# The FFN product with W_base by Strassen's scheme over pairs of row tiles

## The chip, the cores and the metric

The kernel runs on one core of one Trainium2 chip. The metric is device time in microseconds (us) of one execution; lower is better. Before the change three timed runs took 767.62 us in the median (767.52 to 768.48).

Engine names below: PE is TensorE (matmul and transpose, PEld its weight loads), DVE is VectorE, ACT is ScalarE, POOL is GpSimd, SP is SyncE, which issues nearly all DMAs.

## The reference

One pre-norm transformer block on x of shape (2, 1024, 1024), float32: 2048 tokens, 1024 features.

```
x = x + attn(layernorm(x))        # convolution over 3 tokens -> q, k, v of width 256; 16 heads of 64;
                                  # causal softmax inside blocks of 128 tokens; wo; proj_w to 1024
x = x + ffn(layernorm(x))

ffn(x):  y      = x @ W_base.T + b_base                       # (2048 x 1024) @ (1024 x 1024)
         z_e    = x @ lora_A[e].T            (r = 8)          # for the 4 active experts
         logits = x @ router_W.T + router_b, active ones only
         alpha  = softmax(log(prior + eps) + logits)
         y      + sum_e alpha_e * 2 * (z_e @ lora_B[e].T)
```

The change is in the product with W_base and in what surrounds it.

## The kernel before

Every large product is made of three matmuls: each float32 operand is split into a rounded part "hi" and a rest "lo" (type fp32r), and hi·hi, hi·lo and lo·hi are added in PSUM. The helper `three` (matmul on L140) does this, so most matmuls of the trace carry the line L140 and are told apart by their tiles. A split costs one ACT copy (hi) and one DVE subtraction (lo).

The stages follow each other on PE: layer norm and transposes (tiles `xt`, `tr`), the convolution (`pm`), attention (`pq`, `pv`, scores `s`, transposes `pt`, `po`, `pw`), then the FFN stage. Attention works on 32 head pairs i, two at a time, in 16 rounds K of some 17 us. The FFN stage works on 16 row tiles g of 128 tokens in the order of the list `gs`, n being the place in it. For each tile:

- `load_xr` (DMA of x, 512 KB), `add_projb` (POOL, L1111), `project` (12 matmuls into `pp`), `residual` (DVE, L1126), statistics and `x_norm` (DVE, POOL for the root on L1136, DVE L1141), `transpose_x` (8 transposes `trx`, L1148), `x_hi` (ACT, L1155) and `x_lo` (DVE, L1159): this gives the split transposed tile `xT`, [128 features, 8 chunks, 128 tokens].
- `dense`: 8 chunks dc of 128 features, times three matmuls, times three column ranges of 354, 354 and 352 columns (`CUTS`): 72 matmuls into three PSUM banks `py`. The 1060 columns are the 1024 outputs and, in front of them, 36 columns for the four experts' lora_A rows and router row, so that z and the logits come out of the same matmuls.
- the gate (`gate_logits`, `gate_exp`, `gate`: small DVE and ACT operations), `transpose_z` (`pzt`, L1218), `z_out`, then `experts` (L1232): one matmul per column range adds lora_B and b_base.
- `add_y` (DVE, L1239) adds each bank to the row tile `xr`, and `store` writes it out.

W_base is needed in split form, 1060 columns by two parts for each of the 8 chunks. Six chunks are split during attention (rounds 12 to 14: `staged_hi` on L1071, `staged_lo` on L1075) and kept in DRAM (`wbd`); once the big buffers of attention are free (`big`, `wr0`, `wr1`), `load_staged` (L1083) reads them back, 1 MB each. The last two chunks are split at the start of the FFN stage. All eight stay in SBUF to the end.

The order of work on each engine is fixed when the program is built: every step is an `Op` with an engine, an estimated duration, a due time, the steps it comes after, and the buffers it takes and gives back (`places`: `m` are the 8 PSUM banks, `ml`, `t2`, `t4`, `a4`, `vh` are pools in SBUF). `trace()` plays this plan through and emits the steps in the order of their planned starts. On the chip each engine and SP's DMA queue then work strictly in that order.

Of the kernel before, what the change touches and what calls it, by code (L numbers as in the profile page):

```python
# [10 lines left out]
F32 = mybir.dt.float32  # L11
# [10 lines left out]
P = 128  # L22
# [17 lines left out]
def preln_block_kernel(  # L40
# [70 lines left out]
    BIG = max(NDC * N * (2 * J + 1), 2 * NWC * 2 * HD, 4 * 2 * (ZC + O))  # L111
# [481 lines left out]
    WR = max(2 * NWC * HD, 2 * 2 * (ZC + O))  # L593
# [454 lines left out]
    wb, wb_at = {}, {}  # L1048

    def open_wb(tag, dcs):  # L1050
        k = len(dcs)
        n = 2 * k * (ZC + O)
        t = big("wb0", (n,), FR) if tag == "big" else wr(tag, f"wb_{tag}")[:, :n]
        t = t.rearrange("p (h c f) -> p h c f", h=2, c=k)
        for c, dc in enumerate(dcs):
            wb[dc] = [t[:, h, c, :] for h in range(2)]
            wb_at[dc] = t, c

    def wb_hi(dc, h):
        nc.scalar.copy(wb[dc][0][:, ds(ZC + h * TC, TC)], raw["wb", dc, h])  # L1060

    def wb_lo(dc, h):
        hi, lo = (t[:, ds(ZC + h * TC, TC)] for t in wb[dc])
        nc.vector.tensor_tensor(lo, raw.pop(("wb", dc, h)), hi, ALU.subtract)


    wbd = [dram.tile([P, 2, O], F32, name=f"wbd{dc}") for dc in range(NDC - 2)]

    def staged_hi(dc, h):
        raw["hi", dc, h] = ml(f"wbhi_{dc}_{h}")[:, :TC].bitcast(FR)  # L1070
        nc.scalar.copy(raw["hi", dc, h], raw["wb", dc, h])  # L1071

    def staged_lo(dc, h):
        r = raw["wb", dc, h]
        nc.vector.tensor_tensor(r.bitcast(FR), r, raw["hi", dc, h], ALU.subtract)  # L1075

    def store_staged(dc, h, part):
        t = raw.pop((("hi", "wb")[part], dc, h))
        nc.sync.dma_start(wbd[dc][:, part, ts(h, TC)], t.bitcast(F32) if part == 0 else t)

    def load_staged(dc):
        tag, c = wb_at[dc]
        nc.sync.dma_start(tag[:, :, c, ZC:].bitcast(F32), wbd[dc])  # L1083

    za = ap_.tile([P, 2, EA, NDC * RA], FR, tag="za", name="za", bufs=1)

    def za_hi():
        nc.scalar.copy(za[:, 0], asel[:, :, : NDC * RA])

    def za_lo():  # L1090
        nc.vector.tensor_tensor(za[:, 1], asel[:, :, : NDC * RA], za[:, 0], ALU.subtract)

    def wz(dc):
        t, c = wb_at[dc]
        for h in range(2):
            nc.scalar.copy(
                t[:, h, c, :ZC].rearrange("p (e r) -> p e r", e=EA),
                za[:, h, :, ds(dc * RA, RA)],
            )
# [4 lines left out]
    xrs, xns, xTs, pps, trxs, mvs, rss, pys, zrs, zTs, pzts, gat = ({} for _ in range(12))  # L1104

    def load_xr(g):
        xrs[g] = a4(f"xr_{g}", (D,))
        nc.sync.dma_start(xrs[g], xr_of[g])
# [43 lines left out]
    def x_hi(g, h):  # L1152
        if h == 0:
            xTs[g] = [a4(f"xT{i}_{g}", (NDC, P), FR) for i in range(2)]
        nc.scalar.copy(xTs[g][0][:, ts(h, 4), :], trxs[g, h])  # L1155

    def x_lo(g, h):
        hi, lo = (t[:, ts(h, 4), :] for t in xTs[g])
        nc.vector.tensor_tensor(lo, trxs.pop((g, h)), hi, ALU.subtract)  # L1159


    CUTS = [(0, 354), (354, 708), (708, ZC + O)]
    LAST_CUTS = [(0, 402), (402, 804), (804, ZC + O)]

    def cut(n, k):
        return (LAST_CUTS if n == len(gs) - 1 else CUTS)[k]

    def dense(n, k, dcs):
        g = gs[n]
        a, b = cut(n, k)  # L1170
        if 0 in dcs:
            pys[g, k] = bank(f"py_{g}_{k}", (b - a,))
        for dc in dcs:
            three(
                pys[g, k],
                [t[:, dc, :] for t in xTs[g]],
                [t[:, a:b] for t in wb[dc]],
                dc == 0, k == 0 and dc == NDC - 1,
            )


    def gate_logits(g):
        pz = pys[g, 0][:, :ZC].rearrange("p (e r) -> p e r", e=EA)
        lg, al, a2 = (
            small.tile([P, EA], F32, tag=t, name=f"{t}_{g}") for t in ("lg", "al", "a2")
        )
        nm, asum, ar = (
            small.tile([P, 1], F32, tag=t, name=f"{t}_{g}") for t in ("nm", "asum", "ar")
        )
        nc.vector.tensor_tensor(lg, pz[:, :, R], lbias, ALU.add)  # L1190
        nc.vector.tensor_reduce(nm, lg, AX.X, ALU.max, negate=True)  # L1191
        gat[g] = pz, lg, al, a2, nm, asum, ar

    def gate_exp(g):
        pz, lg, al, a2, nm, asum, ar = gat[g]
        nc.scalar.activation(al, lg, AF.Exp, bias=nm, accum_out=asum)  # L1196

    def gate(g):
        pz, lg, al, a2, nm, asum, ar = gat.pop(g)
        nc.vector.reciprocal(ar, asum)  # L1200
        nc.vector.tensor_scalar(a2, al, ar, LORA_SCALING, ALU.mult, ALU.mult)
        zs = small.tile([P, ER], F32, tag="zs", name=f"zs_{g}")
        nc.vector.tensor_tensor(
            zs.rearrange("p (e r) -> p e r", r=R),
            pz[:, :, 0:R],
            a2[:, :, None].to_broadcast([P, EA, R]),
            ALU.mult,
        )

        zr = zrs[g] = small.tile([P, ZK], FR, tag="zr", name=f"zr_{g}")  # L1210
        nc.vector.memset(zr[:, 3 * ER :].bitcast(F32), 1.0)
        nc.vector.tensor_copy(zr[:, ts(0, ER)], zs)
        nc.vector.tensor_tensor(zr[:, ts(1, ER)], zs, zr[:, ts(0, ER)], ALU.subtract)
        nc.vector.tensor_copy(zr[:, ts(2, ER)], zs)

    def transpose_z(g):
        pzts[g] = bank(f"pzt_{g}", (P,), FR, rows=ZK)
        nc.tensor.transpose(pzts[g], zrs.pop(g), identr)  # L1218

    def z_out(g):  # L1220
        zTs[g] = small.tile([ZK, P], FR, tag="zT", name=f"zT_{g}", bufs=2)
        nc.scalar.copy(zTs[g], pzts.pop(g))

    def y_part(n, k):

        a, b = cut(n, k)
        py = pys[gs[n], k]
        return (py[:, ZC:], 0, b - ZC) if k == 0 else (py, a - ZC, b - ZC)

    def experts(n, k):  # L1230
        py, a, b = y_part(n, k)
        nc.tensor.matmul(  # L1232
            py, zTs[gs[n]], bb[:ZK, a:b], start=False, stop=True, skip_group_check=k == 0
        )

    def add_y(n, k):
        py, a, b = y_part(n, k)
        x2 = xrs[gs[n]]
        nc.vector.tensor_tensor(x2[:, a:b], py, x2[:, a:b], ALU.add)  # L1239
        pys.pop((gs[n], k))  # L1240

    def store(n, k=None):
        g = gs[n]
        a, b = (0, O) if k is None else (max(0, cut(n, k)[0] - ZC), cut(n, k)[1] - ZC)
        nc.sync.dma_start(or_of[g][:, a:b], xrs[g][:, a:b])
# [6 lines left out]
        m=[0.0] * 8, t2=[0.0] * 6, t4=[0.0] * 6, a4=[0.0] * A4, ml=[0.0] * 2, vh=[0.0] * 2  # L1252
# [97 lines left out]
    def plan_x(n, due):  # L1350
        g = gs[n]
        op(("X", n), DMA, 1.4, due - 12.0, [], partial(load_xr, g), lag=3.0, need=("a4",))
        op(("xb", n), POOL, 2.4, due - 4.0, [("X", n), ("pb",)], partial(add_projb, g))

    def plan_p(n):
# [3 lines left out]
        if ch < NCHUNK - 2 and g % NB == 0:  # L1359
            for wc in range(NWC):  # L1360
                op(("oh", ch, wc), DMA, 1.4, at[0] - 6.0, [("os", ch, wc)], partial(load_oh, ch, wc),
                   lag=3.0, need=("t4",))
                d["ol", ch, wc] = d["oh", ch, wc]
        for h in range(2):
            pe(("P", n, h), MM,
               [("ol", ch, wc) for wc in range(NWC)] + [("rl", "pw", wc, h) for wc in range(NWC)],
               partial(project, g, h), give=("t4",) * 2 if h and g % NB == NB - 1 else ())
# [6 lines left out]
    def plan_tx(n):  # L1374
        g = gs[n]
        for h in range(2):
            pe(("TX", n, h), 0.44, [("xn", n)], partial(transpose_x, g, h),
               give=("a4",) if h else ())
            op(("xh", n, h), ACT, 0.55, at[0] + 0.5, [("TX", n, h), ("xh", n, 0)],
               partial(x_hi, g, h),  # L1380
               need=("a4",) * 2 if h == 0 else ())
            op(("xl", n, h), DVE, 0.65, at[0] + 1.2, [("xh", n, h)], partial(x_lo, g, h),
               give=("m",))

    def after_dense(n, k, dc):
        return [("xl", n, dc // 4), ("rl", "wb", dc, 0), ("rl", "wb", dc, 1), ("wz", dc, 1)] + (
            [("Y", n, k, dc - 1)] if dc else [])

    def plan_dense(n, k, dcs):
        a, b = cut(n, k)  # L1390
        for dc in dcs:
            pe(("Y", n, k, dc), 3 * (b - a) * 0.000454, after_dense(n, k, dc),
               partial(dense, n, k, [dc]), need=("m",) if dc == 0 else (),
               give=("a4",) * 2 if (k, dc) == (2, NDC - 1) else ())
# [226 lines left out]
```

## Time and profile before

| | |
|---|---|
| median of three runs | 767.62 us |
| the profiled execution | 767.54 us, of which its span is 765.5 us |
| granted TensorE clock in it | 0.999 |
| PE busy | 756.6 us |
| DVE busy | 545.0 us |
| ACT busy | 400.5 us |
| POOL busy | 157.8 us |
| DMA | 100.19 MB, mean 131 GB/s |
| FFN stage, from the first `py` matmul to the end | 515.84 to 765.5 us |

The span runs from the first to the last instruction of the program. A group's busy time is the union of its instructions' times. A matmul's own duration contains its way through the array and overlaps the next one, so what one matmul costs is read from the time between starts (the chain of waits gives it for runs of equal matmuls). An engine can be busy all the time and still not be at its peak.

### The profile page before, as it was taken

To read this page: it belongs to the slowest core of one execution; us is meant where nothing else is said; L and a number is where in the kernel's file an instruction comes from. 1 tells how busy PE (TensorE), PEld (TensorE's weight loads), DVE (VectorE), ACT (ScalarE), POOL (GpSimd) and SP (SyncE) were. 2 spreads that over 40 slices of the span, in tenths; PEclk is the share of its full clock that TensorE was granted. 3 is DMA by queue.
4 is the path that set the end of the run, shared out by engine and by line. 5 is a ranking of instruction groups with operands and counts; after the bars stand their busy time and mean duration, and the time that the engine had idled before them with its cause. 6 is when DMAs were issued, how large, how long until landed. Compare 5 with 4: busy or idle time off the path is not lost.

```text
span 765.5 us, 13108 instructions
## 1 busy us (share of the span) xinstructions
PE 756.6 (99%) x4948; PEld 676.6 (88%) x4948; DVE 545.0 (71%) x1027; ACT 400.5 (52%) x1015; POOL 157.8 (21%) x138
## 2 busy tenths in 40 slices
PE   7999999999999999999999999999999999999998
PEld 7999988888888888888888887889999999999998
DVE  7888899889766998878887788687434454444532
ACT  6987337364837978887787989832101101010110
POOL 3224222210000322212122113442121111221000
PEclk9999999999999999999999999999999999999999
DMA  8937994994831121031031646750313112311011
GB/s 343 365 104 229 238 259 124 292 272 116 284 118 56 42 63 41 2 118 42 23 97 50 201 166 218 277 213 21 110 56 111 56 56 102 118 56 56 29 56 56
DMA packets 53663, 100.19 MB, mean 131 GB/s; under 512 B 4526, under 2 KB 23742, under 8 KB 53600
## 3 DMA queue, kind: packets, MB, share of 16 engines
q1 hardware_dynamic: 49872, 89.35, 33.2%
q0 software_dynamic: 3728, 10.00, 7.3%
q8 instruction: 39, 0.64, 0.3%
q14 instruction: 24, 0.20, 0.1%
HBM read 73.12 MB, written 26.21 MB: 130 GB/s over the span
## 4 chain that ended last, share of the span: by engine, by line
PE 95%; DVE 2%; DMA 1%; ACT 1%; issue 0%; POOL 0%; DVEq 0%
PE pm L140 26%; PE py L140 25%; PE pq L140 11%; PE pp L140 6%; PE pw L140 5%; PE pv L140 5%; PE s L904 4%; PE po L968 4%; PE pt L951 4%; PE trx L1148 2%; PE tr L385 1%; PE py L1232 1%; DVE lnst L132 1%; DMA xt<-in_x 1%; DMA wbd<-raw_wb 0%; DMA raw_pw<-in_proj_w 0%
## 5 line engine op out<-in xcount | busy, mean ns | idle before, releaser
L140 PE MATMUL pm<-v,u 128*128 128x256 f32 (+1 forms) x1152 | 203.1, 337 | 1.3 <-ACT v L473 0.9
L140 PEld LDWEIGHTS pm<-v,u 128*128 128x128 f32 x1152 | 177.9, 190 | 24.2 <-ACT v L473 1.2
L140 PE MATMUL py<-wb,xT 128*128 128x354 f32 (+3 forms) x576 | 120.4, 327 | 0.0
L140 PE MATMUL py<-wb_wr,xT 128*128 128x354 f32 (+3 forms) x576 | 118.1, 327 | 0.0
L944 POOL TENSOR_TENSOR p<-p,rs 128x1024 f32<-128x1024 f32 x32 | 61.5, 1926 | 251.5 <-DVE rs L940 204.0
L933 ACT ACTIVATE p<-p,nmx 128x128 f32<-128x128 f32 x256 | 99.4, 397 | 2.6 <-DVE nmx L928 2.5
L140 PEld LDWEIGHTS py<-wb_wr,xT 128*128 128x128 f32 x576 | 96.6, 188 | 2.4
L140 PEld LDWEIGHTS py<-wb,xT 128*128 128x128 f32 x576 | 96.6, 189 | 0.1
L140 PE MATMUL pq<-yt,wqk 128*128 128x512 f32 x384 | 94.3, 399 | 0.0
L140 PEld LDWEIGHTS pq<-yt,wqk 128*128 128x128 f32 x384 | 70.7, 188 | 18.4 <-issue 1.5
L1159 DVE TENSOR_TENSOR xT<-trx,xT 128x512 fp32r<-128x512 f32 x32 | 20.9, 686 | 56.0 <-PE trx L1148 49.1
L1155 ACT CAST xT<-trx 128x512 fp32r<-128x512 f32 x32 | 18.6, 588 | 63.7 <-POOL xr L1111 31.9
L1196 ACT ACTIVATE al<-lg,nm 128x4 f32<-128x4 f32 x16 | 4.8, 297 | 88.0 <-DVE nm L1191 88.0
L1111 POOL TENSOR_TENSOR xr<-xr,projb 128x1024 f32<-128x1024 f32 x16 | 38.4, 2398 | 60.1 <-DMA xr<-in_x 59.4
L933 ACT ACTIVATION_READ_ACCUMULATOR p<-p,nmx 128x1 f32 x256 | 50.0, 195 | 0.0
L919 DVE TENSOR_TENSOR p<-s,mask 128x512 f32<-128x512 f32 x64 | 41.6, 677 | 8.8 <-PE s L904 8.6
L140 PE MATMUL pw<-oT,wot 128*128 128x512 f32 x192 | 47.6, 396 | 0.0
L140 PE MATMUL pv<-wvt,yt 128*128 128x512 f32 x192 | 46.6, 392 | 0.0
L896 ACT ACTIVATE qk<-pq,bq 128x512 f32<-128x512 f32 x32 | 37.8, 1182 | 13.6 <-PE pq L140 13.6
L140 PEld LDWEIGHTS pw<-oT,wot 128*128 128x128 f32 x192 | 35.9, 188 | 8.5
L140 PEld LDWEIGHTS pv<-wvt,yt 128*128 128x128 f32 x192 | 36.1, 188 | 8.2
L445 DVE TENSOR_TENSOR u<-g,u 128x768 fp32r<-128x768 f32 x40 | 37.5, 951 | 1.4 <-ACT u L441 1.2
(161 smaller groups left out, 1196.4 us busy)
## 6 DMA issues: line engine op xcount, KB each, us to landing
g<-in_conv_w SPq DMA_DIRECT2D x48, 384.0 KB, 7.6
mdr<-m SPq DMA_DIRECT2D x36, 256.0 KB, 3.1
g<-in_conv_w POOLq DMA_DIRECT2D x24, 384.0 KB, 7.7
xt<-in_x SPq DMA_DIRECT2D x16, 512.0 KB, 9.7
xr<-in_x SPq DMA_DIRECT2D x16, 512.0 KB, 3.9
out<-xr SPq DMA_DIRECT2D x15, 512.0 KB, 2.9
ml<-mdr SPq DMA_DIRECT2D x18, 384.0 KB, 3.5
raw_wb<-in_w_base SPq DMA_DIRECT2D x16, 256.0 KB, 9.6
```

The costliest lines, as they stand in the source:

```text
L140: nc.tensor.matmul(ps, l[a], r[b], start=first and i == 0, stop=last and i == 2)
L445: nc.vector.tensor_tensor(lo, raws.pop((v, dc)), hi, ALU.subtract)
L896: nc.scalar.activation(out, pq, AF.Identity, bias=b_ap[:, hp : hp + 1], scale=sc)
L904: nc.tensor.matmul(s[j][:, b, :], qh[ts(j, DH), ts(b, P)], kh[ts(j, DH), ts(b, P)], start=True, stop=True,)
L919: nc.vector.tensor_tensor(ps[i][0][:, ts(j, NB), :], ss[i][j], mask[:, None, :].to_broadcast([P, NB, P]), ALU.add,)
L933: nc.scalar.activation(p[:, k, :], p[:, k, :], AF.Exp, bias=nmx[:, k : k + 1], accum_out=sm[:, k : k + 1],)
L944: nc.gpsimd.tensor_tensor(p, p, rs[:, :, None].to_broadcast([P, 2 * NB, P]), ALU.mult)
L951: nc.tensor.transpose(pt[:, ts(b, P)], ps[i][0][:, j * NB + b, :], ident)
L968: nc.tensor.matmul(po[ts(j, DH), ts(b, P)], vh[:, b, ds((i % 4) * P + j * DH, DH)], pT[:, j, ts(b, P)], start=True, stop=True,)
L1111: nc.gpsimd.tensor_tensor(xrs[g], xrs[g], pwt["b"], ALU.add)
L1155: nc.scalar.copy(xTs[g][0][:, ts(h, 4), :], trxs[g, h])
L1159: nc.vector.tensor_tensor(lo, trxs.pop((g, h)), hi, ALU.subtract)
```

## The change

The product of two row tiles (256 tokens, 1024 features) with W_base (1024 features, 1024 outputs) is cut into 2 by 2 blocks: A11, A12 are the first tile's two halves of features, A21, A22 the second's; B11 to B22 are the blocks of the weights, 512 by 512. Strassen's scheme (in Winograd's form) takes seven block products instead of eight, with sums of A blocks (S1 to S4) and differences of B blocks (T1 to T4). The stage now steps over eight pairs m.

- Each product is two half products of 6 matmuls, all 512 columns wide (`multiply_half`): 84 matmuls for a pair into the banks a, b, c, e. The products are A11·B11, S2·T2, A12·B21, S1·T1, S3·T3, S4·B22, A22·T4, in that order.
- S1 to S4 are made by DVE from the transposes in PSUM; A21 is copied to SBUF by ACT; seven operands of a pair are split (before: two tiles, four halves).
- The banks are combined: `u_first` copies bank a (ACT), `u_second` adds b (DVE), POOL adds the sum to three half rows of `xr` (`add_u`), and DVE adds bank e and bank c once more in the middle of their accumulation (`add_y` with last=False).
- z and the logits have products of their own (`z_products`): 32 matmuls for a pair with 72 or 36 weight columns and 128 moving columns, a copy to SBUF (`z_keep`), and two matmuls that add the two parts and turn the result (`z_turn`). The gate works on two tiles at once. `experts` is four matmuls of 512 columns for a pair.
- Weights: the 28 units (T1 to T4, B11, B21, B22, four chunks each, 128 by 512) are split during attention and kept in DRAM (`wsd`). T's are made by POOL (`stage_add`, 16 operations of 128x512) in rounds 1, 4, 6 and 9; B11, B21, B22 are staged in rounds 11 to 14. In the FFN stage B11 and T2 lie in `big`, T1 in `wr0`, T4 in `wr1`, T3 in eight small tiles; B21 and B22 are read from DRAM for each pair, two loads of 1 MB each, into the two `vh` buffers (`stream`).
- `xr` takes buffers of the pool `t4` in place of `a4`, one buffer of `a4` is lent to the staging of the T's, and `plan_x` asks for its load later (6 us before its due time in place of 12, from the fifth tile on).

The diff, cut to its core:

```diff
-    wbd = [dram.tile([P, 2, O], F32, name=f"wbd{dc}") for dc in range(NDC - 2)]
+    wsd = {
+        (n, h): dram.tile([P, 2, 2, TC], F32, name=f"wsd_{n}_{h}")
+        for n in ("B11", "B21", "B22", "T1", "T2", "T3", "T4") for h in range(2)
+    }
...
+    def stage_add(k, a, b, how):
+        nc.gpsimd.tensor_tensor(raw[k], raw[a], raw[b], how)
...
+    def load_half(n, h):
+        if n in ("B21", "B22"):
+            t = ap_.tile([P, NB, 512], F32, tag="vh", name=f"wb_{n}_{h}_{len(wb)}")
+            wb[n, h] = halves(t.rearrange("p b f -> p (b f)").bitcast(FR))[0]
+        nc.sync.dma_start(wb[n, h].bitcast(F32), wsd[n, h])
...
+    def sum_s(m, n):
+        g0, g1 = gs[2 * m : 2 * m + 2]
+        a, b, how = {
+            "S1": (trxs.get((g1, 1)), s_of(m, "S3"), ALU.add),
+            "S2": (s_of(m, "S1"), trxs.get((g0, 0)), ALU.subtract),
+            "S3": (trxs.get((g0, 0)), s_of(m, "S3"), ALU.subtract),
+            "S4": (trxs.get((g0, 1)), s_of(m, "S2"), ALU.subtract),
+        }[n]
+        nc.vector.tensor_tensor(s_of(m, n), a, b, how)
...
+    def op_hi(m, n):
+        nc.scalar.copy(operand(m, n)[:, 0], source(m, n))
+
+    def op_lo(m, n):
+        nc.vector.tensor_tensor(opd[m, n][:, 1], source(m, n), opd[m, n][:, 0], ALU.subtract)
...
-    def dense(n, k, dcs):
...
+    def multiply_half(m, k, h):
+        o, w, b, opens = PRODUCTS[k]
...
+        for c in (2 * h, 2 * h + 1):
+            l, r = [opd[m, o][:, i, c, :] for i in range(2)], weight(w, c)
+            for i, (x, y) in enumerate(((0, 0), (0, 1), (1, 0))):
+                nc.tensor.matmul(
+                    pys[m, b], l[x], r[y], start=opens and c == 0 and i == 0,
...
+    def z_products(m):
+        pz = pys[m, "z"] = bank(f"pz_{m}", (2, P), rows=2 * ZC)
+        for t, parts in enumerate((((("A11", 0), ("A12", NH)), (("S1", 0), ("A22", NDC))))):
+            for j, (o, a) in enumerate(parts):
+                for c in range(NH):
+                    for i in range(2):
+                        rows = (2 - i) * ZC
+                        nc.tensor.matmul(
+                            pz[:rows, t],
+                            zw[:, a + c].rearrange("p h z -> p (h z)")[:, :rows],
+                            opd[m, o][:, i, c, :],
...
+    def z_turn(m):
+        pys[m, "z"] = bank(f"pzs_{m}", (2, ZC))
+        for t in range(2):
+            nc.tensor.matmul(pys[m, "z"][:, t], gat[m][:, t], zsum, start=True, stop=True)
...
+    def add_u(m, t):
+        x2 = xrs[gs[2 * m + t]].rearrange("p (h f) -> p h f", h=2)
+        if t == 0:
+            nc.gpsimd.tensor_tensor(x2[:, 1], x2[:, 1], u2s[m], ALU.add)
+        else:
+            nc.gpsimd.tensor_tensor(
+                x2, x2, u2s.pop(m)[:, None, :].to_broadcast([P, 2, TC]), ALU.add
             )
...
+    DIFFERENCES = (1, 4, 6, 9)
+    todo = [(n, c) for n in ("B11", "B21", "B22") for c in range(NH)]
+    SPLITS = {K: todo[3 * i : 3 * i + 3] for i, K in enumerate((11, 12, 13, 14))}
...
+    for m in range(NM):
+
+        more = m + 1 < NM
+        if more:
+            plan_p(2 * m + 3)
+        plan_product(m, 1)
+        if more:
+            plan_p(2 * m + 2)
+        plan_product(m, 6)
+        stream(m, "B21")
+        plan_product(m, 2)
+        if more:
+            for h in range(2):
+                plan_tx(m + 1, 1, h)
+        plan_product(m, 5)
+        plan_zs(m)
+        plan_product(m, 7, [partial(plan_gate, m)])
+        if more:
+            for h in range(2):
+                plan_tx(m + 1, 0, h)
+        stream(m, "B22")
+        plan_product(m, 3)
+        plan_z(m)
+        plan_e(m, 0, 0, "a", [("Y", m, 2, 1)])
+        plan_e(m, 0, 1, "e", [("Y", m, 3, 1)])
+        plan_e(m, 1, 1, "f", [], True)
...
```

As built, PE's order within a pair in the steady state is: S2·T2 and A12·B21 in alternating halves, the transposes of the next pair's second tile, S1·T1 and S3·T3 in alternating halves, `z_products`, the transposes of the next pair's first tile, `z_turn`, S4·B22 and A22·T4 in alternating halves, the gate's transposes `pzt`, half a projection, the four `experts` matmuls, half a projection, and A11·B11 of the next pair between the halves of another projection. In the last pair `pzt` and the four `experts` matmuls are the last work of PE.

## The prediction

> **What bounds the kernel now.** I read the page's busy line and slices first, then the chain of waits, then the chain in order of time, which prices each kind of matmul, then windows of the stages, and last single rows.
>
> ```profile
> PE 756.6 (99%) x4948; PEld 676.6 (88%) x4948; DVE 545.0 (71%) x1027; ACT 400.5 (52%) x1015; POOL 157.8 (21%) x138
> ...
> PE   7999999999999999999999999999999999999998
> ...
> DVE  7888899889766998878887788687434454444532
> ...
> PE 95%; DVE 2%; DMA 1%; ACT 1%; issue 0%; POOL 0%; DVEq 0%
> ```
>
> PE is busy all the way and 95% of the chain lies on it: the span is the sum of PE's matmuls. DVE has about half of its time free in the FFN stage (the last third of the slices) and little before it. So the change is worth what it takes off PE, less any wait that it makes.
>
> ```profile
> 393.38 1.75 PE pt L951 x16
> ...
> 487.66 1.90 PE po L968 x32
> ...
> 516.09 11.62 PE py L140 x72
> ...
> 560.51 2.77 PE pp L140 x12
> ```
>
> These are the prices (start, us, what, count). One tile's dense product is 72 matmuls in 11.62 us: 161.4 ns each, 354 columns wide. A 512-column fp32r matmul of the same stage takes 2.77/12 = 231 ns. So a column costs 0.456 ns in the narrow ones and 0.451 ns in the wide ones: width alone gains nothing. A matmul of 128 moving columns takes 1.90/32 = 59 ns with 64 weight columns (`po`) and 1.75/16 = 109 ns with 128 (`pt`).
>
> ```profile
> 259.00:276.00 17.00, 17.00 (x124) 14.29 (x124) 16.93 (x31) 13.24 (x43) 3.88 (x2) 1.00 0.20 59
> ...
> 446.00:463.00 17.00, 16.35 (x121) 13.34 (x120) 13.53 (x20) 14.99 (x48) 5.04 (x3) 1.00 0.56 183
> ...
> 480.00:497.00 17.00, 17.00 (x140) 14.44 (x140) 10.94 (x18) 14.96 (x69) 8.02 (x4) 1.00 0.76 294
> ...
> 582.05:598.11 16.06, 16.06 (x97) 15.30 (x97) 7.59 (x23) 1.83 (x5) 2.94 (x3) 1.00 0.37 132
> ```
>
> Columns: length, then busy PE, PEld, DVE, ACT, POOL, clock, DMA share, GB/s. The last row is one row tile: 16.06 us, all PE, DVE 7.59. The first is attention with DVE full (16.93 of 17). The second has one of PE's rare idle times. The third shows DMA at 294 GB/s.
>
> **PE in the FFN stage, per pair of tiles.** Removed: 144 dense matmuls, 2 x 11.62 = 23.24; six `experts` matmuls, 0.59 per tile by the starts of their rows in the timeline (0.25 + 0.17 + 0.17) = 1.18. Added: 84 matmuls of 512 columns at 231 ns = 19.39; four `experts` of 512 columns = 0.92; `z_turn`, two matmuls with 128 weight columns at 109 ns = 0.22; and 32 in `z_products`, a shape that the trace lacks (72 and 36 weight columns by turns, 128 moving). Its bounds are 59 ns (`po`) and 109 ns (`pt`). The mean weight width of 54 is nearest to `po`, so I take 60 ns: 1.92, with 3.49 as the upper end. Projections, transposes and `pzt` stay. Sum: 24.42 - 22.45 = 1.97 us per pair, 15.8 us for eight. So seven products for eight do not give an eighth of 238 us (the two `py` groups' busy times, which overlap each other: the chain gives 16 x 11.62 = 186). They give 16 x 11.62 - 8 x 19.39 = 30.8, and half of that goes to z, which rode along before for 36 of 1060 columns.
>
> The Trainium skill, page "TensorE: Matmul & The Clock Gate", section "Back-to-back issue gap", gives about 81 ns for a matmul of 128 columns in a stream with weight loads and 131 ns for 512; the row above has 231 ns for 512 columns, so for that width the trace contradicts it. With its 81 ns `z_products` would be 2.59 per pair and the kernel 5.4 us later than my sum, by that estimate from the page.
>
> **The other engines in the FFN stage.** DVE per pair by the rows: 4 `residual` x 0.69, 4 half statistics x 0.64 with 4 small rows (0.72), 2 `x_norm` x 0.80, 7 lo splits x 0.69, 4 sums x 0.69, `u_second` and the two early `add_y` x 0.69, 4 last `add_y` x 0.69, gate 1.9: some 22 us of a pair's 30, against 15.2 of 32.1 before. ACT gets 8 copies of 0.59 and four small ones, 6 us. POOL gets `add_u`, 2.40 (the row of `add_projb`, same size) and about 1.2 (half of it), beside two `add_projb` and two roots: 9.5 us. None is the bound, and I price them at nothing as long as PE's order gives them time. Going through that order with these durations, the tightest place is `pzt`: between `z_turn` and `pzt` PE has 24 matmuls = 5.5 us, in which DVE must do two sums, two splits and the gate in order, with ACT's exp behind four casts: about 4.6. Slack 0.9 us. The second is the next pair's last transposes, which come behind `add_u` and the root on POOL: 1.5 to 2 us of slack. `z_keep` (0.4 and a handover) lies under 8 transposes (0.87). The waits inside a bank's accumulation are hidden too: A12·B21 waits for `u_first` (0.59), with two halves (2.8) of PE work between; S4·B22 and A22·T4 wait for the early `add_y` (0.69), with `z_products`, transposes and more (over 3) between. If that cover went, PE's queue would stand still for the copy, since it is in order.
>
> DMA per pair: 4 MB of B21 and B22 beside 2 MB of x and out and 0.5 MB of attention output, 6.8 MB (10^6) in 30 us = 226 GB/s, below the 294 of the window above. SP works in order: a `stream` load waits for its `vh` buffer, and the x loads and out stores queued behind wait with it. From release to use PE has other work: for B22 two halves (2.8), transposes (0.87), four halves (5.5), `z_products` (1.9), transposes (0.87), 12 us; for B21 three halves, a projection in two parts, `experts`, and A11·B11 with a second projection, some 15; 1 MB landed here in
>
> ```profile
> wb<-wbd SPq DMA_DIRECT2D x4, 1024.0 KB, 14.8
> wb_wr<-wbd SPq DMA_DIRECT2D x2, 1024.0 KB, 6.2
> ```
>
> 6.2 us with two queued, 14.8 with four. `stream` queues two, so I take 6.2: hidden.
>
> **Attention.** 28 units are split in place of 16 (12 staged, 4 at the stage's start): 16 new ones in rounds 1, 4, 6, 9 with 0.69 us DVE, 0.62 us ACT, one read and two stores of 256 KB each, and 16 POOL operations at about 1 us (half of the 1.90 of `normalized`, which waits behind them). SP gets some 48 more issues of 0.33 us; the `ml<-mdr` loads of the next tokens stand behind stores that wait for a split, and need the same two `ml` buffers. Rounds 11 to 14 get 3 units each where 12 to 14 had 4, which is a little relief. DVE has 34 us idle from 225 to 412 (153.0 busy of 187 in the windows), but 259 to 276 is full and round 1 falls on it. POOL work also slows DVE:
>
> ```profile
> 453.95 1.90 POOL L944 TENSOR_TENSOR p<-p,rs 128x1024 f32<-128x1024 f32 x1 [13.54 <-DVE rs L940]
> ...
> 454.81 2.20 DVE L1075 TENSOR_TENSOR raw_wb<-raw_wb,wbhi 128x512 fp32r<-128x512 f32 x2
> ```
>
> Two subtractions of 0.69 took 2.20 while POOL multiplied. I charge PE 2 us, with 0 and 8 as ends (8 is round 1's four units, 2.8, plus four held up by 1.2).
>
> The Trainium skill, page "SBUF — State Buffer", section "SBUF: two separate sides", says that a DVE operation with two SBUF inputs and a GpSimd operation exclude each other for the whole instruction. That speaks against moving sums to POOL; by it each of six such DVE operations of a pair (four S splits, two `x_norm`) could lose up to 2.40 us, where the rows above show 0.8 for two. On DVE's 8 us of slack the forecast stands either way.
>
> **Both ends of the stage.** At the start some 12 MB must be loaded (before: 6 and four raw quarters) between the end of attention's use of `big` (last `pq` at 475.6) and the middle of the first pair (about 535): 60 us at 294 GB/s carry 17 MB. Hidden, but SP's queue is tight; I charge 1 us, ends -1 and 4. At the end `pzt`, ACT's `zT` (0.27 and handovers, 0.6), four `experts` and four adds of 0.69 on DVE come after the last dense matmul, then the store:
>
> ```profile
> 761.79 0.28 PE L1232 MATMUL py<-bb,zT 98*128 98x256 f32 x1
> ...
> 762.12 0.43 DVE L1239 TENSOR_TENSOR xr<-py,xr 128x256 f32<-128x256 f32 x1 [0.60 <-PE py L1232]
> ```
>
> Before, 3.4 us lie between the last add's start and 765.5. After: 0.7 (pzt, zT) + 0.23 + 0.2 + 4 x 0.69 + 3.0 = 6.9 from the last dense matmul, against 3.7 + 0.3 before, and 1.0 of it is in the pair's sum: 2.2 us more.
>
> **Sum.** 767.54 (span 765.5 and 2.0 around it; the median of the runs, 767.62, is the same) - 15.8 + 2.2 + 2 + 1 = 757 us.
>
> **Rivals.** (1) Slower, by the gate. If `pzt` comes late in each pair, since one of DVE's queued operations is held for a POOL operation (2.40) and a further 0.9 is lost in DVE's longer queue, PE waits 2.4 us behind the slack of 0.9, eight times: 757 + 19 = 776. It decides from 10.6/8 = 1.3 us per pair. For it: DVE's load in the stage rises from 47% to 73%, and the row that shows the hold. Against: no POOL work is due there by PE's order. (2) Attention pays: all 16 units' 0.69 us come through to PE (11 us in place of 2): 766, about no change. For: the full window; against: 34 us idle around it. (3) z at 109 ns: +12.5, 769.5. For: `pt` has the same moving width; against: its weights are 128 wide. (4) Streams land as late as 14.8: B22 waits 2.8 per pair, 779.
>
> **How the numbers follow.** Forecast 0.62 (its own range 750 to 763: 241 ns for 512 columns, as `pq` has, gives +6.7, 227 ns gives -2.7, ends of attention and start -3 to +6); (2) 0.13, half of it within 0.2%; (3) 0.07; (1) 0.13; (4) 0.05. A measurement can tell about 0.2% (1.5 us). Faster 0.69, same 0.08, slower 0.23. 748 to 774 leaves out (4), half of (1) and a few in a hundred below.
>
> **What would show it.** Right: 84 matmuls of 231 ns and 32 of about 60 ns per pair, a pair in some 30 us with PE without gaps, attention ending within 2 us of its old time. Wrong: idle time before `pzt`, `pz` starts 109 ns apart, `py` waiting for a DMA of `wb_B`, or PE gaps in rounds 1 to 5.

## The result, and the profile after

The changed kernel takes 759.66 us (median of 4 runs, 758.48 to 760.12) against 767.84 us (4 runs, 767.52 to 768.48): ratio 0.989, 95% interval 0.9873 to 0.9907. That is 8.2 us saved, where 10.6 had been forecast. The profiled execution took 760.05 us with a span of 758.3 us.

The page of the changed kernel: busy times, slices, chain.

```profile
PE 744.3 (98%) x4740; PEld 634.7 (84%) x4740; DVE 604.3 (80%) x1050; ACT 422.0 (56%) x1028; POOL 213.0 (28%) x170
...
DVE  7888899889766899999899988789666767567652
...
PE 82%; DVE 9%; ACT 6%; DMA 1%; issue 1%; SPq 0%; DVEq 0%; ACTq 0%
```

PE is still the bound, but its share of the chain fell from 95% to 82%, and DVE's rose from 2% to 9%. The DVE slices tell where: in attention (the 13th to 28th) they now read mostly 8 and 9 where 7 and 8 stood, in the FFN stage behind it 5 to 7 where 3 to 5 stood.

The chain in order of time, in one pair of the FFN stage of the changed kernel (start, us, what):

```profile
550.09 1.39 PE py_a L1262 x6
...
567.65 2.01 PE pz L1279 x32
...
576.55 0.12 PE pzt L1343 x2
```

Half products of 1.39 us (232 ns for a matmul of 512 columns), z at 63 ns a matmul, and nothing but PE between one `pzt` (546.20) and the next (576.55). The window of the next pair (length, then busy PE, PEld, DVE, ACT, POOL, clock, DMA share, GB/s) and the waits of PE (us in total, times, longest; the longest is left out, since it lies at the program's start) agree:

```profile
576.39:606.75 30.36, 30.36 (x167) 25.29 (x166) 21.78 (x44) 6.06 (x12) 9.95 (x6) 1.00 0.62 243
```

```profile
PE s L905 <- ACT vh L873: 2.5, 2, 1.5
PE po L969 <- DVE p L920: 0.7, 1, 0.7
...
PE py_a L1353 <- ACT zT L1347: 0.5, 1, 0.5
```

A pair takes 30.36 us, all of it PE; DVE has 21.78 us to do in it. No product waits for a streamed block, a gate or a sum; the waits lie in attention (`s`, `po`), 0.5 us in the tail (`py_a`), and, as in the kernel before, some ahead of attention. The streams landed in 4.8 us:

```profile
wb_B<-wsd_B SPq DMA_DIRECT2D x32, 1024.0 KB, 4.8
```

Cut at the first `pq` matmul and at the first dense one, the two profiles compare so:

| | before | after |
|---|---|---|
| ahead of attention | 229.58 us | 230.13 us |
| attention, first `pq` to first dense matmul | 286.26 | 289.44 |
| FFN stage, from there to the end | 249.71 | 238.70 |

The stage that was changed gives 11.0 us; attention, where the T's are now made, takes 3.2 back. Nothing of the change lies ahead of attention; that part differs from run to run (229.4 to 232.6 us over the profiles of this study). Five profiles with the same attention code have 288.75 to 289.44 us for it, so 0.7 us is what this cut can't tell.

This is how a T can reach PE. The timeline of the changed kernel, POOL, DVE, ACT and PE rows from 302 to 313 us (start, us, engine, line, operation; in brackets the idle time before it):

```profile
302.11 2.15 POOL L945 TENSOR_TENSOR p<-p,rs 128x1024 f32<-128x1024 f32 x1 [2.15 <-DVE rs L941]
304.22 1.33 POOL L1080 TENSOR_TENSOR pv<-pv_T,pv 128x512 f32<-128x512 f32 x1
305.52 1.94 POOL L945 TENSOR_TENSOR p<-p,rs 128x1024 f32<-128x1024 f32 x1
...
302.54 1.87 DVE L571 TENSOR_TENSOR y<-pq 128x128 f32<-128x128 f32 x1
304.33 1.38 DVE L572 SCALAR_TENSOR_TENSOR y<-pq 128x128 f32<-128x128 f32 x1
305.63 1.98 DVE L573 SCALAR_TENSOR_TENSOR y<-pq 128x128 f32<-128x128 f32 x1
...
308.77 0.40 ACT L934 ACTIVATE p<-p,nmx 128x128 f32<-128x128 f32 x1 [4.24 <-DVE nmx L929]
...
311.87 0.56 ACT L873 COPY vh<-pv 128x512 f32<-128x512 f32 x1
...
312.48 1.48 PE L905 MATMUL s<-qk,qk 64*128 64x128 f32 x16 [1.52 <-ACT vh L873]
```

Three small DVE operations of the token joins (such a one takes 0.28 us when it is left alone; their `pq` is a tile of the join in SBUF, not the PSUM tile that PE writes) last 1.87, 1.38 and 1.98 us: each ends some 0.15 us after the POOL operation that ran when it began (304.41 against 304.26, 305.71 against 305.55, 307.61 against 307.46). Only the middle one of the three POOL operations belongs to a T (L1080); the other two are the softmax's own (L945). Behind them on DVE the maximum `nmx` is late, ACT stands idle for 4.24 us waiting for it, its exponentials come late, and behind these its eviction of `pv`; PE waits 1.52 us for that bank. The same place in t_no_pool, one of the experiments below, which leaves out the POOL operations of the T's and keeps the order of the rest:

```profile
302.69 1.98 DVE L572 SCALAR_TENSOR_TENSOR y<-pq 128x128 f32<-128x128 f32 x1
304.60 0.28 DVE L573 SCALAR_TENSOR_TENSOR y<-pq 128x128 f32<-128x128 f32 x1
...
306.04 0.40 ACT L934 ACTIVATE p<-p,nmx 128x128 f32<-128x128 f32 x1 [2.05 <-DVE nmx L929]
...
310.36 1.16 PE L905 MATMUL s<-qk,qk 64*128 64x128 f32 x16
```

One join fewer is held, ACT stands idle for 2.05 us in place of 4.24, and PE's wait is gone. The Trainium skill, page "SBUF — State Buffer", section "SBUF: two separate sides", says that a DVE operation with two SBUF inputs and a GpSimd operation that reads SBUF shut each other out for a whole instruction; these rows agree.

### The profile page after: what moved, and what is told of

It reads as the page before. It is cut to its first block, busy times and chain, and to the rows that moved or that the text cites. A ratio compares the mean times of both kernels' runs of the same rounds, so it can differ in the third digit from the quotient of the medians.

```text
span 758.3 us, 12914 instructions
## 1 busy us (share of the span) xinstructions
PE 744.3 (98%) x4740; PEld 634.7 (84%) x4740; DVE 604.3 (80%) x1050; ACT 422.0 (56%) x1028; POOL 213.0 (28%) x170
## 4 chain that ended last, share of the span: by engine, by line
PE 82%; DVE 9%; ACT 6%; DMA 1%; issue 1%; SPq 0%; DVEq 0%; ACTq 0%
PE pm L141 26%; PE pq L141 8%; PE py_e L1262 6%; PE pp L141 6%; PE py_a L1262 6%; PE py_c L1262 6%; PE pw L141 4%; PE pv L141 4%; ACT p L934 3%; PE py_b L1262 3%; PE po L969 3%; PE pt L952 2%; PE s L905 2%; PE pz L1279 2%; PE trx L1202 2%; PE tr L386 1%
## 5 line engine op out<-in xcount | busy, mean ns | idle before, releaser
L945 POOL TENSOR_TENSOR p<-p,rs 128x1024 f32<-128x1024 f32 x32 | 64.8, 2025 | 144.8 <-DVE rs L941 120.3
L424 POOL DMA_DIRECT2D g<-in_conv_w x24 | 21.2, 925 | 68.4 <-ACT g L420 36.6
L1240 ACT CAST S<-s 128x512 fp32r<-128x512 f32 x32 | 19.7, 621 | 35.8 <-DVE s L1234 31.5
L929 DVE TENSOR_REDUCE nmx<-p 128x8 f32<-128x1024 f32 x32 | 38.3, 1201 | 0.0
L905 PE MATMUL s<-qk,qk 64*128 64x128 f32 x512 | 34.6, 280 | 3.1 <-ACT vh L873 2.5
L905 PEld LDWEIGHTS s<-qk,qk 64*128 64x128 f32 x512 | 30.9, 187 | 7.6 <-ACT vh L873 3.2
L442 ACT CAST u<-g 128x768 fp32r<-128x768 f32 x40 | 32.5, 837 | 4.8 <-PE pm L141 4.7
L1360 ACT COPY u<-py_a 128x512 f32<-128x512 f32 x8 | 4.7, 588 | 53.0 <-PE py_a L1262 53.0
```

The source lines that it names most:

```text
L442: nc.scalar.copy(us[v, dc][0], raws[v, dc])
L905: nc.tensor.matmul(s[j][:, b, :], qh[ts(j, DH), ts(b, P)], kh[ts(j, DH), ts(b, P)], start=True, stop=True,)
L929: nc.vector.tensor_reduce(nmx, p, AX.X, ALU.max, negate=True)
L945: nc.gpsimd.tensor_tensor(p, p, rs[:, :, None].to_broadcast([P, 2 * NB, P]), ALU.mult)
```

## The experiments

The times of attention and the FFN stage are cut from each kernel's profile as above; the medians have a run of the kernel before beside them on the same chip.

| | median us | ratio to before (95%) | attention | FFN stage |
|---|---|---|---|---|
| after_again | 760.5 | 0.9893 (0.9878 to 0.9908) | 289.41 | 238.70 |
| no_t | 754.25 | 0.9808 (0.9791 to 0.9825) | 282.33 | 238.70 |
| t_no_pool | 756.17 | 0.9856 (0.9835 to 0.9877) | 286.05 | 238.71 |
| t_no_lo | 755.8 | 0.9843 (0.9828 to 0.9858) | 285.30 | 238.71 |
| t_on_dve | 760.92 | 0.9911 (0.9896 to 0.9927) | 289.99 | 238.71 |
| t_rounds | 762.18 | 0.9915 (0.9895 to 0.9934) | 289.83 | 238.70 |
| t_late | 779.12 | 1.0134 (1.0115 to 1.0154) | 292.67 | 257.62 |
| t3_twice | 781.44 | 1.017 (1.0152 to 1.0188) | 289.39 | 260.40 |
| z_quarter | 747.57 | 0.9719 (0.97 to 0.9738) | 288.99 | 226.55 |
| gate_early | 758.04 | 0.9854 (0.9838 to 0.9871) | 288.75 | 236.63 |
| v_on_act | 762.9 | 0.9923 (0.9909 to 0.9936) | 294.96 | 236.63 |
| late_split | 759.09 | 0.9872 (0.9855 to 0.989) | 292.57 | 236.87 |

### What do the T's cost in attention? (no_t, t_no_pool, t_no_lo)

no_t, no staging of the T's at all:

```diff
-        nc.sync.dma_start(wb[n, h].bitcast(F32), wsd[n, h])
+        nc.sync.dma_start(wb[n, h].bitcast(F32), wsd["B11" if n[0] == "T" else n, h])
...
-            plan_differences(DIFFERENCES.index(K), t0 + 6.0)
...
```

> Leaves out the whole staging of the four differences T1 to T4 in the attention stage (16 loads-and-subtractions, 16 splits, their stores); the products that want a T read the stored pieces of B11 in its place, so the FFN stage moves and multiplies exactly as much as before. The trace of the changed kernel has its FFN stage starting at 519.6 us against 515.8 us in the kernel before, so up to 3.7 us net, and about 5.2 us of PE idle by single gaps, were lost in attention. If the staging of T is what costs it (either by GpSimd or by load): 754.0 to 756.5 us, FFN stage starting at 514 to 516.5 us, the 1.5 us gap ahead of the scores at 312 us and the 1.0 us gap at 384 us gone. If it is something else (the twelve splits of B11, B21, B22 in rounds 11 to 14, or the other order of the work): 759 to 760.5 us, as the changed kernel.

Measured 754.25 us, attention 282.33 us and PE without a gap in it. So the staging of the T's costs attention 7.1 us (289.44 - 282.33), more than the 3.2 that the comparison with the kernel before shows: the rest of attention had become 3.9 us shorter at the same time (286.26 before, 282.33 here). The planner fills the places that fall free, so this kernel's order differs as well; the next two keep the order.

t_no_pool, the POOL operations alone left out:

```diff
-               partial(stage_add, (n, c), (a, c), (b, c), how))
+               int)
```

> Leaves out only the sixteen GpSimd instructions that form the differences T1 to T4: loads, splits on ScalarE and VectorE, stores and the order of all the rest stay, and the pieces stored are those of undifferenced blocks. Theory one (GpSimd holds VectorE: while a 1.3 us GpSimd operation runs, a VectorE operation with two SBUF inputs doesn't finish, so the evictions behind it on VectorE and ScalarE are late and PE waits for PSUM): most of the attention loss goes, 754.5 to 757 us, the summed lengthening of VectorE's operations between 225 and 410 us falls from 28 us to about 15 to 18 us. Rival (the sixteen extra splits and transfers load ScalarE and VectorE by 16 x (0.56 + 0.69) us and take staging buffers): the time stays at 759 to 760.5 us.

Measured 756.17 us, attention 286.05 us: 3.4 of the 7.1 us come from the sixteen POOL operations. The time fell as theory one had it, but its second mark failed. The lengthening of DVE's operations between 225 and 410 us (each one's duration above the shortest of its line and shape, summed) fell only from 36.2 to 34.1 us: most of it belongs to the softmax's own POOL operations (L945), which met the token joins in this kernel just as often. So DVE's plain load was tested next.

t_no_lo, the low halves of the T's left out, POOL operations kept:

```diff
-        op(("sl", *k), DVE, 0.66, due - 0.7, [("sh", *k)] + after, partial(staged_lo, *k))
+        op(("sl", *k), DVE, 0.66, due - 0.7, [("sh", *k)] + after,
+           int if n[0] == "T" else partial(staged_lo, *k))
```

> Leaves out only the sixteen VectorE subtractions that make the low parts of T1 to T4 (0.69 us each, 11 us of VectorE): the GpSimd differences, the high parts, all loads and stores and the order of the rest stay, and the low piece stored is the undivided block. In the changed kernel VectorE is busy 93 to 98% between 260 and 460 us. Theory now (VectorE is full in attention, and each us of its time, own or held by GpSimd, delays evictions that PE waits for): 16 x 0.69 us less of it gives back as much as leaving out the GpSimd operations did (3.4 us in the attention stage), 755 to 757.5 us. Rival (only the meeting of GpSimd's operations with VectorE's costs): these stay, so 759 to 760.5 us.

Measured 755.8 us, attention 285.30 us: 4.1 us come back although every POOL operation is still there. The meeting of POOL and DVE alone can't be the cause; DVE's own work costs time as well. The windows from 260 to 460 us show how PE's idle time and DVE's load go together; each line below sums five windows of 40 us (busy time of each engine). First the changed kernel, then no_t, t_no_lo and t_no_pool:

```profile
sum 200.00, PE 195.62 PEld 163.24 DVE 188.19 ACT 167.69 POOL 64.09; mean PE 39.12 PEld 32.65 DVE 37.64 ACT 33.54 POOL 12.82
```

```profile
sum 200.00, PE 200.00 PEld 168.96 DVE 167.15 ACT 167.73 POOL 48.70; mean PE 40.00 PEld 33.79 DVE 33.43 ACT 33.55 POOL 9.74
```

```profile
sum 200.00, PE 198.34 PEld 166.32 DVE 179.54 ACT 172.21 POOL 65.07; mean PE 39.67 PEld 33.26 DVE 35.91 ACT 34.44 POOL 13.01
```

```profile
sum 200.00, PE 198.00 PEld 165.72 DVE 187.26 ACT 170.62 POOL 47.27; mean PE 39.60 PEld 33.14 DVE 37.45 ACT 34.12 POOL 9.45
```

With DVE at 188 of 200 us PE stands idle for 4.4 (200 - 195.62), with 180 for 1.7, with 167 not at all; ACT is at 168 to 172 in all. But DVE's busy time alone does not give the loss. In t_no_pool DVE has 187 and PE loses only 2.0, and in t_on_dve, below, DVE has 192.06 and PE loses 3.4 (200 - 196.64), less than in the changed kernel. So it counts, too, where in its queue DVE is held.

The two parts, 3.4 and 4.1, make up the whole of the 7.1 within what the cut can tell, so sixteen casts on ACT and the transfers seem to cost little; this takes it that the parts simply add, which was not tested. Of the 7.1 us, 4.4 are idle time of PE. In the other 2.7 the same 2100 PE instructions of the stage start further apart (285.06 us in place of 282.33), at the full granted clock; why, is open. The order may have a share of its own: eight joins last over 0.8 us in the changed kernel, seven in t_no_pool and eight in t_no_lo, but only one in no_t and one in the kernel before, whose orders differ.

### Can the differences go elsewhere? (t_on_dve, t_rounds, t_late)

```diff
-        nc.gpsimd.tensor_tensor(raw[k], raw[a], raw[b], how)
+        nc.vector.tensor_tensor(raw[k], raw[a], raw[b], how)
...
-            op(("df", n, c), POOL, 1.3, due + (-2.0, -0.7, 4.0, 10.0)[i], after,
+            op(("df", n, c), DVE, 0.35, due + (-2.0, -0.7, 4.0, 10.0)[i], after,
```

> The complete kernel with the sixteen differences made by VectorE instead of GpSimd (about 0.7 us each, 11 us of VectorE in all, in the same rounds of attention). Theory one (GpSimd's hold on VectorE is the cost): each difference costs VectorE 0.7 us in place of being held up to 1.3 us once or twice, 755.5 to 758.5 us. Rival (VectorE's load in attention is the cost, whoever adds it): 760.5 to 766 us, with longer waits of PE for VectorE's evictions than in the changed kernel.

Measured 760.92 us, attention 289.99 us, the same as with POOL (289.44) within 0.7: the rival's case. PE's waits for DVE's own `vh` rose from 0.3 to 1.6 us, and those for ACT's fell from 2.5 to 1.6. Sixteen operations on DVE cost what sixteen on POOL cost. That POOL's are paid in DVE's busy time is not shown: leaving them out (t_no_pool) took it only from 188.19 to 187.26 us of the five windows.

```diff
-    DIFFERENCES = (1, 4, 6, 9)
+    DIFFERENCES = (3, 5, 7, 9)
```

> The complete kernel with the four groups of differences in rounds 3, 5, 7 and 9 of attention, where one part of the tokens is joined in each round, in place of rounds 1, 4, 6 and 9, of which three join two parts. Theory (the price is the meeting of the GpSimd operations with the joins on VectorE, whose operations then last up to 2 us): fewer meetings, 756 to 758.5 us. Rival (the price belongs to the amount of work, wherever it lies): 759 to 760.5 us.

Measured 762.18 us (759.83 to 764.06), above both expectations; the profiled execution, with 760.8, is one of the shorter ones. Its attention takes 289.83 us: no gain. The gaps only moved (1.3 us at 296, 1.1 at 366 and 1.4 at 453 us). Nor did the edit thin out the meetings: seven joins last over 0.8 us in it, against eight, so it doesn't decide between the two.

```diff
-    DIFFERENCES = (1, 4, 6, 9)
+    DIFFERENCES = (11, 12, 13, 14)
     todo = [(n, c) for n in ("B11", "B21", "B22") for c in range(NH)]
-    SPLITS = {K: todo[3 * i : 3 * i + 3] for i, K in enumerate((11, 12, 13, 14))}
+    SPLITS = {K: todo[3 * i : 3 * i + 3] for i, K in enumerate((2, 4, 6, 8))}
```

> The complete kernel with the two stagings changed about: the splits of B11, B21 and B22, which need no GpSimd, in rounds 2, 4, 6 and 8, and the four groups of differences in rounds 11 to 14, of which only 11 and 12 join a part of the tokens. Theory (meeting of GpSimd operations with the token joins): 755.5 to 758 us, the long VectorE operations of the joins in rounds 4 to 9 gone. Rival (amount of work): 759 to 761 us, the PE gaps only moved to rounds 11 to 14, where projection and lora weights are split too.

Both expectations missed: 779.12 us, slower than before the change. The waits of PE in t_late say why, and a window behind the first of them shows a second loss:

```profile
PE py_b L1262 <- DMA wb<-wsd_T: 6.1, 1, 6.1
PE py_e L1262 <- DVE xr L1376: 5.2, 1, 5.2
```

```profile
549.00:552.00 3.00, 3.00 (x9) 2.42 (x9) 0.15 (x1) 0.37 (x1) 0.00 (x0) 0.50 0.19 46
```

T2, made last, lands 6.1 us after PE wants it in the first pair, and DVE's early addition comes 5.2 us late; idle times in the stage sum to 14.1 us against 0.5. Behind each of the two the granted clock is 0.50 (the figure after POOL's), with 427 ns between matmuls where 232 is usual: for 18 matmuls of `py_b` and `py_e` another 3.5 us. Attention itself took 292.67 us, 5.3 of it idle, so nothing was gained there either.

### Is the FFN stage bound by PE, as the sum has it? (t3_twice, z_quarter)

```diff
-            for i, (x, y) in enumerate(((0, 0), (0, 1), (1, 0))):
+            terms = ((0, 0), (0, 1), (1, 0)) * (2 if k == 7 else 1)
+            for i, (x, y) in enumerate(terms):
```

> Every matmul of the product with T3 is issued twice into the same accumulation (96 matmuls of 512 columns a pair in place of 84, as many as eight block products; only the second addend is wrong, by a doubled c). If PE bounds the FFN stage, each of the 96 added matmuls costs its pitch of 0.2325 us: 8 x 12 x 0.2325 = 22.3 us, 781 to 783 us. Rival (the stage has slack hidden elsewhere, so that the product saved was worth less): under 776 us. That it ends above the time of the kernel before would show what the scheme's side work costs: 16 us of the 22.3 us saved kept in the pair, the rest spent.

Measured 781.44 us; FFN stage 260.40 us, 21.7 more, 226 ns for each of the 96 added matmuls. One of eight products is worth what its matmuls cost, and without the saving the scheme would have lost 13 us to the kernel before.

```diff
-                for c in range(NH):
+                for c in range(1):
```

> Only a quarter of the products that make the gate's z are issued (8 of 32 a pair: the first of the four chunks of each operand), so the gate's values are wrong; all else is as in the changed kernel. The trace of the changed kernel has the 32 at 63 ns each. If they lie on PE's path: -24 x 0.063 x 8 = -12.1 us against the changed kernel, 747 to 749 us. Rival (each pair waits for something else there, such as the next pair's operands or a streamed block, so that taking PE work out uncovers a wait): 752 us or more, with new idle time of PE ahead of the first product of the next pair or of the product with B22.

Measured 747.57 us; FFN stage 226.55 us, 12.15 less, as expected. z is 16 us of pure PE time in this form.

### The tail (gate_early)

```diff
+        if not more:
+            plan_zs(m, True)
         plan_product(m, 2)
...
+        if not more:
+            plan_gate(m)
         plan_product(m, 5)
...
+        if not more:
+            plan_z(m)
+            plan_e(m, 0, 0, "a", [("Y", m, 2, 1)])
         plan_product(m, 3)
```

> The complete kernel; in the last pair alone z's products come before the product with B21, the gate's chain runs during the product with T1, and the transposes of z and the expert products into a, e and f come before the last dense product, with only that into c behind it. In the changed kernel 7.0 us pass from the last dense matmul's end to the end of the span: 0.8 us for the transposes and zT, 0.5 for the first expert product, four additions of 0.69 us and 3.2 us for the last store. Expected: three expert products and the transposes (0.95 us of PE) move ahead of the end of the dense work, one addition in place of four stays behind it: about 0.45 + 0.7 + 3.2 = 4.4 us, so -1.7 us against the changed kernel, 757.5 to 758.5 us. Rival (the tail is set by the stores, which queue behind each other): no gain, 759 to 760 us.

Measured 758.04 us; FFN stage 236.63 us, 2.07 less. The end of the chain in order of time, first of the changed kernel, then of gate_early:

```profile
748.60 2.79 PE py_c L1262 x12
751.39 0.14 PE pzt L1343 x2
...
752.57 1.29 DVE xr L1376 x2
```

```profile
749.62 2.79 PE py_c L1262 x12
752.42 0.24 PE py_c L1353
...
752.68 0.69 DVE xr L1376
```

From the last dense matmul to the end 6.9 us (751.39 to 758.3) became 3.9 (752.42 to 756.3). It gained a little more than expected, and it is the fastest version that computes all: its interval lies wholly below those of the changed kernel's two measurements.

### Two tries to unload DVE (v_on_act, late_split)

v_on_act is gate_early with ten evictions moved:

```diff
-        if b % 2:
+        if b % 2 and not 1 <= G <= 5:
             nc.vector.tensor_copy(vhs[G][:, b, :], pvs.pop((G, b)))
```

> The complete kernel with the early gate of the last pair, and ten evictions of values (v, odd parts of the groups 1 to 5, in rounds 2 to 11 of attention) moved from VectorE (0.69 us) to ScalarE (0.56 us), which is busy 76 to 93% there. Nothing of the differences is touched. If VectorE is what is full: 7 us less on it in the rounds that are full, 1.5 to 3 us off attention against the kernel with the early gate alone (758.0 us): 755 to 756.5 us. Rival (ScalarE is as near to its limit, or the loss is not VectorE's load): 757.5 to 760 us.

Measured 762.9 us, attention 294.96 us: worse than either expectation. DVE did get free (177.33 of 200 us in the five windows), but PE waits longer: 3.6 us in all ahead of `s` for ACT's `vh`, where gate_early has 1.4, and 1.7 us ahead of `pq` for ACT, which gate_early lacks. Two rows of ACT's timeline in v_on_act:

```profile
311.70 0.56 ACT L873 COPY vh<-pv 128x512 f32<-128x512 f32 x1
...
313.72 0.56 ACT L873 COPY vh<-pv 128x512 f32<-128x512 f32 x1
```

Both copies free a bank that PE wants, and ACT, in order, has four exponentials of 0.39 us and their sums between them; the exponentials in front of the first copy had waited 3.4 us for DVE's `nmx`. Behind two such pairs of waits the granted clock was 0.50 for 3.4 us (314.43 to 317.84 and 351.97 to 355.38 us). Of the 6.2 us by which attention is longer than in gate_early 2.5 are idle time of PE, and at half the clock some 3.4 more go in these two stretches (half of their length, an estimate). So DVE's load isn't the whole law: what counts is how long an eviction stands in its queue.

late_split is gate_early with the splits of T3 and T4 behind their loading:

```diff
+        nc.scalar.copy(hi, lo.bitcast(F32))
...
+    def late_lo(n, c):
+        hi, lo = weight(n, c)
+        nc.vector.tensor_tensor(lo, lo.bitcast(F32), hi, ALU.subtract)
...
+        for n, t in (("T3", 6.0), ("T4", 12.0)):
+            op(("ws", n, c, 1), DMA, 0.75, due + t, [("df", "T2" if n == "T3" else "T4", c)],
+               partial(store_staged, (n, c), 1), lag=3.0, give=("pv",))
```

> The complete kernel with the early gate of the last pair, and the splits of T3 and T4 (8 of the 16: 8 x 0.56 us on ScalarE, 8 x 0.69 us on VectorE, and 8 of the 32 stores) moved out of the full rounds of attention: the differences are stored whole, and split after they are loaded back, around the start of the FFN stage, where VectorE is busy 70%. Theory (VectorE is full from 260 to 460 us; taking the sixteen low parts out gave 4.1 us of attention): half of them give about 2 us, and 8 fewer uses of ScalarE and of the staging buffers something more, so -2 to -3.5 us against the kernel with the early gate (758.0 us): 754.5 to 756 us. Rival (the first pair of the FFN stage has no room for 5.5 us more on VectorE, so that its dense products wait): attention shorter by the same 2 to 3.5 us, but the first pair longer by as much or more, 757.5 to 761 us, with PE idle ahead of the product with T3 or T4.

Measured 759.09 us (757.63 to 763.26): no gain over gate_early. In the profiled execution, one of the long ones, attention is 292.57 us, and the loss sits at its very end. POOL, DVE and PE rows of late_split:

```profile
514.04 2.36 POOL L1178 TENSOR_TENSOR xr<-xr,projb 128x1024 f32<-128x1024 f32 x1 [1.17 <-DMA xr<-in_x]
...
514.53 2.41 DVE L1127 TENSOR_TENSOR wb_T<-wb_T,wb_T 128x512 fp32r<-128x512 f32 x1
516.87 1.40 DVE L990 SCALAR_TENSOR_TENSOR oT<-po,bia,oT 128x512 fp32r<-128x512 f32 x2
...
517.66 4.38 PE L141 MATMUL pw<-oT,wot 128*128 128x512 f32 x11 [2.29 <-DVE oT L990]
```

One moved split (0.69 us alone) is held to 2.41 us while POOL adds to `xr`; `oT`, queued behind it, is late, PE waits 2.29 us, and its eleven matmuls behind that take 4.38 us in place of 2.55 (11 x 0.232). The window shows why (the figure after POOL's is the clock):

```profile
518.31:521.72 3.41, 3.41 (x10) 2.67 (x9) 3.41 (x6) 2.44 (x4) 0.00 (x0) 0.50 0.01 5
```

The rival was right in kind (the new place has no room) and wrong in place: the FFN stage grew by 0.24 us only, the loss came before it. The gain in attention was missing too: without these 4.12 us (2.29 and 1.83) it would be 288.45 us, against 288.75 in gate_early, where 2 to 3.5 us less had been expected. Whether the shorter runs (757.6 to 758.2) lack this wait was not seen, since one execution was profiled.

## Why the prediction was right, step by step

- **The pair, -1.97 us.** It is -1.76 (32.12 by the window of one tile, to 30.36). Added matmuls came to 22.87 in place of 22.45: 19.56 for the products (19.39), 2.01 for z (1.92), 0.37 for `z_turn` (0.22; the trace has four instructions there, not two), 0.93 for `experts` (0.92). What was removed was under-counted too: with the 7.48 us that projections, transposes and `pzt` take in the pair after, 24.63 in place of 24.42. Eight pairs: -14.1, not -15.8. This is the larger error, 1.7 us.
- **z at 60 ns, rival (3) at 109.** 63 ns; z_quarter shows that it is paid in full. The choice of `po` as the nearest row held.
- **What lies hidden.** The gate's result was ready 1.3 us ahead of `pzt` in each pair, 1.8 in the last (0.9 reckoned), so rival (1) has nothing: DVE with 21.78 us in a pair is no bound. The remark that the forecast stands either way if six operations are held for 2.40 us each did not follow, since that is 14.4 us against 8 of slack; it was not put to the test, for in the pair shown above the largest hold added 1.2 us. Streams landed in 4.8 us and no product waited, so rival (4) has nothing either.
- **The tail, +2.2.** 6.9 us from the last dense matmul to the end, as worked out. gate_early shows that it was a matter of order, not of the scheme.
- **The start, +1.** 238.70 - 249.71 = -11.0 = -14.1 + 2.2 + 0.9: what is left for it is 0.9.
- **Attention, +2 with 0 to 8.** This is the weak step, though the sum hardly shows it. Measured net +3.2; but the term was argued as the price of the T's, and that is 7.1 us (no_t), near the upper end, hidden by 3.9 us that the rest of attention lost at the same time. "A little relief" was the whole account of that; which part of it comes from three units a round in place of four was not tried. That the net came so near to the 2 charged is luck. Two of the prediction's own signs went against it: attention ended over 2 us later (the first dense matmul at 519.57 in place of 515.84), and PE had gaps in rounds 1 to 5 (1.52 us at 312). The error in the argument: 34 us of DVE idle from 225 to 412 us were read as room. That is a sum over eleven windows, but DVE's queue is in order, and an eviction that stands behind other work is late even where DVE idles soon after. So 11 us of DVE's own work (t_no_lo: 4.1 us of time) and 16 operations on POOL (t_no_pool: 3.4 us) both came through in part. Rival (2) had the mechanism and too high a price: 11 us of work gave 4.1.

In sum -11.0 + 3.2, and 0.55 ahead of attention where nothing was changed, is the 7.3 us between the two spans (765.55 and 758.27). The forecast missed the median by 2.7 us and the profiled execution by 3.1: 1.7 from the pairs, 1.2 from attention, and the rest from small terms.

## What to carry to other kernels

Saving an eighth of the matmuls gave a kernel bound by PE only a third of that (22 us of matmuls against 8.2), since z lost its free ride, the tail grew, and preparing the operands fell on an engine that was nearly full in another stage. Price preparation work in the stage where it runs and by the queue it stands in. Read that engine's busy time there: with VectorE busy for 84% of the five windows PE lost nothing here, with 89 to 96% it lost 1.7 to 5.7 us, though not in that order. And do not expect relief from giving such work to GpSimd: the sixteen differences cost attention the same on either engine (289.44 and 289.99 us). Before more work is moved, put the last tile's side chain ahead of its last dense product: that gave 2 us for nothing.

## What the runs showed of the hardware that was not expected

- A stall of PE can be paid twice. After 2.29 us of idle time in late_split the granted clock was 0.50 from 518.31 to 521.72 us, and matmuls of 512 columns started 427 ns apart in place of 232; after the 6.1 us in t_late it was 0.50 from 546.62 to 563.68 us, past the second wait of 5.2. After the single waits of 1.5 us (changed kernel, 312 us) and 1.8 us (t_late, 642 us) it stayed at the full rate. After two waits, of 1.6 and 0.9 us within 3.6 us (v_on_act, 314 us) and of 1.2 and 0.5 us within 2.3 us (the same run, 352 us), it was 0.50 for 3.4 us. The Trainium skill, page "TensorE: Matmul & The Clock Gate", section "Part 1: The HAM clock gate (the "warmup" mystery)", puts the half clock behind at least one idle window of about 3.4 us; here less idle time was enough, and the measurement decides.
- A DVE operation that met a POOL operation ended only after it: joins of 0.28 us alone ended some 0.15 us after POOL's and lasted up to 1.98 us, a split of 0.69 us alone ended 0.54 us after POOL's and lasted 2.41.
